# Attention weights: scores computed twice, places in rows, maxima subtracted by a product

## The chip, the cores and the metric

The kernel runs on one core of a Trainium2 chip. Its time is the device time of one execution in microseconds. Before the change the median of three runs is 446.92 us (446.77 to 449.26). The core's engines have their own instruction queues and run beside each other, held together by semaphores: PE (TensorE, matrix products and transposes into PSUM), DVE (VectorE), ACT (ScalarE), POOL (GpSimd) and SP (SyncE, which issues DMAs).

## The reference, cut to what matters

Sixteen batches of 128 rows and 128 features attend to a context of 77 places with 96 features, in 16 heads of 8. Then each row goes four times through two of four experts. All is float32.

```python
def _L0_xattn_ref(x, y, Wq, bq, Wkv, bkv, Wo, bo):      # x: (16, 128, 128), y: (16, 77, 96)
    q = (jnp.einsum('bld,ed->ble', x, Wq) + bq).reshape(b, l, h, dh)         # h = 16, dh = 8
    kv = (jnp.einsum('bmc,ec->bme', y, Wkv) + bkv).reshape(b, m, h, 2 * dh)
    k, v = (kv[..., :dh], kv[..., dh:])
    att = jax.nn.softmax(jnp.einsum('blhd,bmhd->blmh', q, k) * scale, axis=2)
    out = jnp.einsum('blmh,bmhd->blhd', att, v).reshape(b, l, d)
    return jnp.einsum('bld,ed->ble', out, Wo) + bo
...
x = x + jnp.tanh(g_xattn[0]) * _L0_xattn_ref(_layernorm(x, axis=-1), ctx_768, ...)
x = x + jnp.tanh(g_ffn[0]) * _L0_ffn_ref(_layernorm(x, axis=-1), ...)   # 4 rounds, top 2 of 4 experts
```

## The kernel before

There are two stages. The attention runs over the 16 batches `b`, one round of a loop for each (from L1072). Then the expert layers run over the rows in two halves and four rounds (`phase`, L1169), after the rows of a half were sorted by their experts: they are stored one tile at a time by indirect DMAs from POOL (`scatter`, L511) and loaded again by SP (`load`, L529). The first half is batches 0 to 7; its routing (`gate`, `count`, `route`, `places`) is spread over rounds 7 to 11, its eight stores over rounds 11 to 14, each held behind a DVE instruction of a list named `beats`.

The order on PE, DVE and ACT is the order of the program text (L80). POOL's own steps called through `gp` keep the program's order too. So each engine works through its instructions in line, and an instruction that waits holds up all behind it on its engine.

A round of the loop before:

- `spread_keys` (L765) on POOL, two batches ahead: the keys of a batch, 128 features by 77 places, times a mask, so that `km` holds four copies, each with one head of four left in (128 x 308).
- `turn_weights` (L816): the weights `ex`, query rows by heads and places, are transposed on PE head by head (16 transposes, 128x77 to 77x128, into `ps_tr`), and ACT copies each four of them to `exT`. It is called for groups 0 and 1, then after the next batch's scores for groups 2 and 3.
- `scores` (L778) of the next batch: four products, each on 32 of the 128 rows of PE, two to a PSUM tile of two banks (`sc`).
- Extra steps from lists by round (L953 to L976): for the next group of four batches `turn_ctx` (transposes of the context), `keys`, `turn_x` (transposes of the normalised rows), `queries` and `values`. `early` steps stand before the scores, `extra` ones behind them, `behind` ones at the round's end.
- `weights` (L797): for each half of the heads DVE takes the maximum over the places (`mx`) and subtracts it (`ex`), ACT takes the exponential.
- `put_out` (L848) of the batch before: the output projection into `ps_o`, and its sum with the residual on DVE.
- `attend` (L823): into `ps_av`, half 0 the sums of the weights (by `one`), half 1 the weighted values (by `vm`), each as four products in turn for each of four column groups, with the 77 places as PE's rows.
- `over_sums` (L841): a reciprocal and a product on DVE.

PSUM has eight banks: `p_m` two of one bank (L103), used by `ps_av` and the extra steps; `p_tr` two of one bank, used by `ps_tr` and `ps_o`; `p_sc` two tiles of two banks for the scores. A tile that takes a buffer waits until the reads of the tile before in it are done.

Ahead of the loop (L859 to L896) the first batches are prepared; `warm` and `warm_tr` are products of zeros in between.

## Time and profile before

| what | us |
|---|---|
| time, median of three runs | 446.92 |
| the profiled execution's own time | 444.04 |
| its span, first to last instruction | 442.3 |
| PE busy | 427.3 (97%) |
| DVE busy | 343.7 (78%) |
| ACT busy | 275.7 (62%) |
| POOL busy | 216.7 (49%) |
| 256 transposes of weights on PE, `ps_tr` | 35.1, 280 ns each with overlap |
| 64 copies of them on ACT, `exT` | 34.0, 582 ns each |
| 32 maxima on DVE, `mx` | 25.3, 790 ns each |
| 32 subtractions on DVE, `ex` | 25.4, 794 ns each |
| 32 exponentials on ACT, `ex` | 22.8, 718 ns each |

The granted clock is 0.993 of full speed over the span. Busy times are sums over the whole span, and a PE instruction is shown longer than the time until the next can start, so the sum of its durations is more than its busy time. First attend: 17.2 us after the start; the last begins at 107.4 us; the first product of the expert layers stands at 110.97 us. The stages have different limits, so the chain of waits (what released each step, followed back from the end) is read by stage.

### The profile page before, as it was taken

What the parts mean: (1) busy time and instruction counts of PE and PEld (TensorE: products, weight loads), DVE (VectorE), ACT (ScalarE), POOL (GpSimd) and SP (SyncE); (2) the same over time, 40 slices, a digit from 0 to 9 for tenths busy, and PEclk for the clock granted to TensorE, in tenths of its full rate; (3) what the DMA queues carried; (4) which work ended last, traced back from release to release, by engine and by line L of the source; (5) the groups of instructions that cost most, each with busy time, mean ns of one, the idle gap of its engine ahead of it and who ended that gap; (6) DMA issues with size and microseconds to landing.
All of it is one profiled execution on the core that took longest, in us unless ns stands there. A gap on an engine that the chain in (4) does not pass through costs nothing.

```text
span 442.3 us, 12215 instructions
## 1 busy us (share of the span) xinstructions
PE 427.3 (97%) x4492; PEld 403.8 (91%) x4492; DVE 343.7 (78%) x918; ACT 275.7 (62%) x857; POOL 216.7 (49%) x251
## 2 busy tenths in 40 slices
PE   9899999998999999999999999999999999999991
PEld 8678788876999999999999999999999999999991
DVE  7599989999667996887698589758867986764561
ACT  3677766756565666666566656656666665666661
POOL 6197824174025915852682475258326814650061
PEclk9999999999999999999999999999999999999997
DMA  6520000014002301400130131023011301400010
GB/s 164 189 99 3 3 1 1 4 63 136 2 27 75 99 1 63 137 2 26 66 108 1 50 99 50 1 76 124 1 37 63 100 2 63 146 31 9 1 33 16
DMA packets 19711, 24.08 MB, mean 54 GB/s; under 512 B 4099, under 2 KB 16708, under 8 KB 19524
## 3 DMA queue, kind: packets, MB, share of 16 engines
q1 hardware_dynamic: 15444, 13.43, 9.7%
q0 software_dynamic: 3584, 9.70, 6.2%
q8 instruction: 36, 0.59, 0.6%
q10 hardware_dynamic: 624, 0.17, 0.2%
q14 instruction: 23, 0.19, 0.1%
HBM read 13.58 MB, written 9.71 MB: 53 GB/s over the span
## 4 chain that ended last, share of the span: by engine, by line
PE 72%; issue 9%; DVE 9%; POOL 6%; DMA 2%; ACT 1%; POOLq 0%; DVEq 0%; SPq 0%; ACTq 0%
PE ps_y L255 28%; PE ps_h L255 28%; POOL out_dram L1156 4%; PE ps_av L255 3%; PE ps_tr L258 3%; DVE mx L803 2%; DVE ex L807 2%; PE ps_c L258 2%; DVE rs L843 1%; PE sc L255 1%; PE ps_warm L255 1%; PE ps_bh L255 1%; DMA rows<-sorted 1%; DMA sorted<-rows,pos_i 1%; POOL rows L93 1%
## 5 line engine op out<-in xcount | busy, mean ns | idle before, releaser
L1128 ACT ACTIVATE hT<-ps_h,wb 128x128 f32<-128x128 f32 x512 | 146.4, 369 | 81.2 <-ACT hT L1128 56.4
L255 PE MATMUL ps_h<-curT,wb 128*128 128x128 f32 x1024 | 135.4, 275 | 0.7 <-ACT curT L372 0.7
L255 PE MATMUL ps_y<-wb,hT 128*128 128x128 f32 x1024 | 135.7, 276 | 0.0
L255 PEld LDWEIGHTS ps_h<-curT,wb 128*128 128x128 f32 x1024 | 124.6, 192 | 0.9 <-ACT curT L372 0.9
L515 POOL DMA_INDIRECT sorted<-rows,pos_i x64 | 70.0, 1093 | 112.2 <-DVE start L508 49.3
L255 PEld LDWEIGHTS ps_y<-wb,hT 128*128 128x128 f32 x1024 | 124.5, 192 | 0.0
L1048 DVE COPY wb<-wall 128x1028 f32 x128 | 104.7, 820 | 13.1 <-issue 6.8
L93 POOL TENSOR_TENSOR lp<-rows,wg_rows 128x512 f32<-128x512 f32 x48 | 75.2, 1592 | 29.8 <-DVE rows L1142 27.3
L1142 DVE SCALAR_TENSOR_TENSOR rows<-ps_y,pws,rows 128x128 f32<-128x128 f32 x126 | 43.6, 346 | 34.0 <-PE ps_y L255 34.0
L1128 ACT ACTIVATE hT<-ps_h,wall 128x128 f32<-128x128 f32 x160 | 45.7, 368 | 32.5 <-PE ps_h L255 32.5
L255 PE MATMUL ps_y<-wall,hT 128*128 128x128 f32 x320 | 43.1, 278 | 0.0
L255 PE MATMUL ps_h<-cx,wall 128*128 128x128 f32 x320 | 42.3, 275 | 0.0
L821 ACT COPY exT<-ps_tr 77x512 f32<-77x512 f32 x64 | 34.0, 582 | 12.2 <-PE ps_tr L258 11.9
L255 PEld LDWEIGHTS ps_y<-wall,hT 128*128 128x128 f32 x320 | 38.9, 192 | 2.7 <-ACT hT L1128 2.7
L255 PEld LDWEIGHTS ps_h<-cx,wall 128*128 128x128 f32 x320 | 38.9, 192 | 0.0
L258 PEld LDWEIGHTS ps_tr<-ident,ex 128*77 128x77 f32 x256 | 27.9, 147 | 11.0 <-ACT exT L821 8.4
L258 PE MATMUL ps_tr<-ident,ex 128*77 128x128 f32 x256 | 35.1, 280 | 2.1 <-ACT exT L821 2.1
L1156 POOL DMA_INDIRECT out_dram<-res,id_i x16 | 18.6, 1160 | 35.8 <-DVE res L1147 31.8
L412 DVE TENSOR_REDUCE lg<-lp 128x4 f32<-128x512 f32 x48 | 32.3, 674 | 3.6 <-POOL lp L93 3.6
L813 ACT ACTIVATE ex<-ex 128x616 f32<-128x616 f32 x32 | 22.8, 718 | 13.7 <-DVE ex L807 13.5
L803 DVE TENSOR_REDUCE mx<-sc 128x8 f32<-128x616 f32 x32 | 25.3, 790 | 2.5 <-PE sc L255 2.5
L807 DVE TENSOR_TENSOR ex<-sc,mx 128x616 f32<-128x616 f32 x32 | 25.4, 794 | 1.4
(181 smaller groups left out, 450.5 us busy)
## 6 DMA issues: line engine op xcount, KB each, us to landing
rows<-sorted SPq DMA_DIRECT2D x16, 528.0 KB
wall<-in_L_ffn_W_dram SPq DMA_DIRECT2D x1, 1024.0 KB
wall<-in_L_ffn_W_dram SPq DMA_DIRECT2D x4, 256.0 KB
wg_rows<-wg_turned SPq DMA_DIRECT2D x1, 1024.0 KB
sorted<-rows,pos_i POOLq DMA_INDIRECT x64, 2.7
x_sb<-in_x_dram SPq DMA_DIRECT2D x3, 256.0 KB
ctx_sb<-in_ctx_dram SPq DMA_DIRECT2D x4, 115.5 KB
out_dram<-res,id_i POOLq DMA_INDIRECT x16, 2.3
```

Source lines behind the costliest of these rows:

```text
L93: return lambda *a, **kw: tc.keep_in_program_order(f(*a, **kw))
L255: nc.tensor.matmul(*args, **kw)
L258: nc.tensor.transpose(*args)
L412: nc.vector.tensor_reduce(lgs[h][:, t, :], prods.pop((h, t)), AX.X, ALU.add)
L515: ins = nc.gpsimd.indirect_dma_start(out=sorted_rows[h], out_offset=bass.IndirectOffsetOnAxis(ap=pos_i[:, t : t + 1], axis=0), in_=rows[h] ...
L803: beats.append(nc.vector.tensor_reduce(mx, sv, AX.X, ALU.max))
L807: nc.vector.tensor_tensor(eu.rearrange("l (g h) m -> l g h m", h=HG), sv, mx.unsqueeze(3).to_broadcast([P, 2, HG, M]), ALU.subtract,)
L821: nc.scalar.copy(exT[:, ts(g, HG), :].rearrange("m h l -> m (h l)"), ps[:M, :])
L1048: nc.vector.tensor_copy(wb, wall[:, ds(e, 1), :].rearrange("p o n -> p (o n)"))
L1128: nc.scalar.activation(hT[:, fc, :], ps[:, ts(fc, P)], AF.Gelu_apprx_tanh, bias=wb[:, W_B + fc : W_B + fc + 1],)
L1142: return nc.vector.scalar_tensor_tensor(at, y, w, at, ALU.mult, ALU.add)
L1156: ins = nc.gpsimd.indirect_dma_start(out=out_rows, out_offset=bass.IndirectOffsetOnAxis(ap=id_i[:, t : t + 1], axis=0), in_=res, in_offset ...
```

## The change

The weights are no longer subtracted and transposed. The scores are computed once as before, query rows by places, and only their maxima are taken (`maxima`), into a 128x128 tile `mxs` in which the heads of a group stand at columns 32 g. One transpose (`turn_maxima`, `ps_mx`) and a copy give `mxT`. Then `weights` computes the scores again with places in PSUM's rows, and a second product into the same sum, of a matrix `less` of minus ones and zeros with `mxT`, takes the maxima off. ACT takes the exponentials from PSUM straight into `exT`.

The 77 places are split into 64 and 13. The first 64 of two heads make 128 rows; the other 13 of eight heads make 104 rows (`values_left`, `vr`, `one_r`). So `attend` has three products in turn for each column group instead of four. The context's transpose `ctxT` is kept in two buffers for one group of four batches and holds the first 64 places twice and the last 13 eight times (two copies on ACT); `values` makes eight copies instead of four.

The pool `p_tr` is gone, `p_sc` has three tiles instead of two, and `ps_o` and `ps_mx` are taken from `p_m`. The maxima are taken two batches ahead of attend instead of one, `spread_keys` three ahead, and extra steps move by up to a round.

```diff
-    p_tr = scope.enter_context(tc.tile_pool(name="p_tr", bufs=2, space=PSUM))
-    p_sc = scope.enter_context(tc.tile_pool(name="p_sc", bufs=2, space=PSUM))
+    p_sc = scope.enter_context(tc.tile_pool(name="p_sc", bufs=3, space=PSUM))
...
+    def values_left(i, ps=None, eng=None):
+        if ps is None:
+            ps = bank("ps_vr")
+        for j in range(BB):
+            mm(ps[: HR * MR, ts(j, D)], ctxT[i % 2][:, j, 2 * MP : CT], wvT, ...)
+        v = ps[: HR * MR, :].rearrange("m (b d) -> m b d", d=D)
+        if eng is None:
+            eng = gp
+            left = awork.tile([HR * MR, BB, D], F32, tag="left", name="left", bufs=1)
+            nc.scalar.copy(left, v)
+            v = left
+        eng.tensor_tensor(vr[i % 2], v, one_r.unsqueeze(1).to_broadcast(...), ALU.mult)
...
     def scores(b, km):
...
-                mm(sc[:, g, : HG * M], q[at, :], km[at, :, :]..., start=True, stop=True)
+                dst = sc[:, g, : HG * M].rearrange("l (h m) -> l h m", m=M)
+                left = HG * MP + g * HG * MR
+                for m0, m1, lo in ((0, MP, 0), (MP, M, left)):
+                    mm(dst[:, :, m0:m1], q[at, :], km[at, lo : lo + HG * (m1 - m0)]..., ...)
...
+    def maxima(b, scs, then=None):
+        mx = mxs[b % 2].rearrange("l (t c) -> l t c", c=GW)
+        for u, sc in enumerate(scs):
+            if u and then:
+                then()
+            beats.append(nc.vector.tensor_reduce(mx[:, ts(u, 2), 0:HG], sc..., AX.X, ALU.max))
+
+    def turn_maxima(b):
+        ps = bank("ps_mx")
+        tp(ps[:, :L], mxs[b % 2], ident)
+        mxT = awork.tile([P, L], F32, tag="mxT", name="mxT")
+        nc.scalar.copy(mxT, ps[:, :L])
+        return mxT
+
+    def weights(b, km, mxT):
+        q = qT[b // BB][:, ts(b % BB, L)]
+        scs = [banks2("scT") for _ in range(2)]
+        def product(dst, at, cols):
+            mm(dst, km[at, cols], q[at, :], start=True, stop=False)
+            mm(dst, less[at, cols], mxT[at, :], start=False, stop=True)
+        for j in range(HP):
+            for half in range(2):
+                for g in range(NG):
+                    at = slice(g * GW, (g + 1) * GW)
+                    cols, dst = ts(j, P), scs[g // 2][:, g % 2, ts(j, L)]
+                    if half == 0:
+                        mm(dst, km[at, cols], q[at, :], start=True, stop=False)
+                    else:
+                        mm(dst, less[at, cols], mxT[at, :], start=False, stop=True)
+        n = HR * MR
+        for u in range(2):
+            product(scs[u][:n, 0, ts(HP, L)], slice(u * P // 2, (u + 1) * P // 2), slice(KW - n, KW))
+        exT = awork.tile([P, 2 * TB + 2 * L], F32, tag="exT", name="exT")
+        for u, sc in enumerate(scs):
+            nc.scalar.activation(exT[:, ts(u, TB)]..., sc[:, :, 0 : HP * L], AF.Exp, scale=scale)
+            nc.scalar.activation(exT[:n, 2 * TB + u * L : ...], sc[:n, 0, ts(HP, L)], AF.Exp, scale=scale)
+        return exT
...
     for b in range(B):
-        if b + 2 < B and b + 2 not in kms:
-            kms[b + 2] = spread_keys(b + 2)
-        exT = awork.tile([M, NH, L], F32, tag="exT", name="exT")
-        turn_weights(ex[b], exT, (0, 1))
+        if b + 3 < B:
+            kms[b + 3] = spread_keys(b + 3)
+        if b + 1 < B:
+            exTs[b + 1] = weights(b + 1, kms.pop(b + 1), mxT)
         for f in early[b]:
             f()
-        if b + 1 < B:
-            scs = scores(b + 1, kms.pop(b + 1))
-        turn_weights(ex.pop(b), exT, (2, 3))
+        if b + 2 < B:
+            scs = scores(b + 2, kms[b + 2])
         for f in extra[b]:
             f()
 
         def put_before(b=b):
             if b:
-                put_out(b - 1, o.pop(b - 1), bank_tr)
+                put_out(b - 1, o.pop(b - 1), bank)
 
-        if b + 1 < B:
-            ex[b + 1] = weights(scs, put_before)
+        if b + 2 < B:
+            maxima(b + 2, scs, put_before)
...
-        ps_av = attend(b, exT)
+        ps_av = attend(b, exTs.pop(b))
...
         o[b] = over_sums(ps_av)
+        if b + 2 < B:
+            mxT = turn_maxima(b + 2)
```

Ahead of the loop the changed kernel also makes `less` and the masks for 13 places, and takes the maxima of batches 0 and 1, the weights of batch 0, and the values of the first group, these by DVE instead of ACT. The steps `spread_rows` and `residual(0)` move behind the normalisation of the second group in round 0. The expert layers are the same text.

## The prediction

> **What bounds the kernel now.** I read the page's busy shares first, then cut the span where the work changes, because the change touches only the attention. That is what runs up to about 111 us; after it come the expert layers, which the change leaves alone. The table by stretch (busy us and instruction counts of PE, PEld, DVE, ACT and POOL, then the granted clock):

> ```profile
> 0.00:24.00 24.00, 20.77 (x200) 17.36 (x200) 16.75 (x44) 12.68 (x32) 10.09 (x23) 1.00 0.58 163
> 24.00:61.00 37.00, 36.99 (x632) 29.98 (x635) 34.50 (x77) 26.79 (x55) 26.91 (x82) 1.00 0.09 31
> 61.00:101.00 40.00, 39.32 (x630) 31.76 (x622) 37.29 (x95) 26.29 (x51) 18.27 (x21) 1.00 0.07 23
> 111.00:442.00 331.00, 322.19 (x2888) 318.38 (x2888) 246.16 (x687) 203.49 (x711) 156.63 (x121) 0.99 0.15 51
> ```

> At most 111 of 442.3 us can change. There PE and DVE are both near full, so which one ends a round has to be read from the chain of waits. From 24 to 61 us it is PE, without a gap; one round (batch 5):

> ```profile
> 43.71 1.03 PE ps_tr L258 x8
> 44.74 0.73 PE sc L255 x8
> 45.47 1.03 PE ps_tr L258 x8
> 46.50 0.52 PE ps_k L255 x2
> 47.02 0.22 PE ps_o L255 x2
> 47.24 1.91 PE ps_av L255 x64
> ```

> The reader is to see a round of 5.44 us that is PE work only: 4.92 for the batch and 0.52 for keys. From about 70 to 101 us the chain is DVE's instead:

> ```profile
> 83.85 0.72 DVE mx L803
> 84.61 0.04 issue
> 84.66 0.80 DVE ex L807
> 85.46 0.71 DVE mx L803
> 86.17 0.26 DVE rows L852
> 86.42 0.70 DVE ex L807
> ...
> 87.54 0.85 DVE rs L843
> ```

> A round there is 5.85 us (the chain's ps_av reciprocal stands at 81.69 and 87.54). At the end the first half's rows must be stored, sorted and loaded before the expert layers can begin:

> ```profile
> 102.06 3.54 DMA sorted<-rows,pos_i
> 105.74 3.86 DMA rows<-sorted
> 109.60 0.04 issue
> 109.64 0.67 PE ps_c L258 x4
> ```

> The last attend ends at 110, so these 7.4 us are covered almost exactly.

> **What goes.** Durations from here on are means of the costliest groups, shapes kept apart. Per batch: 16 transposes, 2.06 us of PE; four exT copies of 0.58, 2.3 us of ACT; two subtractions of 0.79, 1.6 us of DVE. DVE's round of 5.2 (two maxima, two subtractions, reciprocal 0.94, oT 0.29, rows 0.34, statistics 0.46) falls to 3.6 and bounds nothing any more. Attend falls from 16 rounds of four column groups to 12: 1.91 x 12/16 = 1.43.

> **What comes, one round on PE.** The maxima's transpose takes 0.27 to its end, its copy on ACT 0.27 (the 128x128 copy of wqT), hand-overs 0.1: the first product with the maxima starts 0.64 after the previous attend, with four score products in its shade. Three more groups of four products follow, two passes each. Four row groups side by side took 0.73 for two passes of 308 columns, 0.15 for one of 128: 6 x 0.15 = 0.9. The products for the left 13 places use half the rows: 8 passes, by ps_o's 0.11 a pass 0.44 (halves side by side) to 0.88 (in line); I take 0.55, and 0.1 for each change of shape (ps_av's 64 passes at 0.11 for each four make 1.75 of its 1.91). Sum 2.2. The scores for the maxima are now 64 + 13 places: 16 passes instead of 8. They also lose half of their neighbours: p_sc has three buffers for four tiles a round, so the second half of the scores takes the banks of the first weights tile and waits for its two exps. Each half is then two row groups alone: two passes of 256 columns and two of 52, by ps_k's 0.26 for 308 columns and a floor of 0.11: 0.65, with the switch 0.75. The exps start when the left product is through, last 0.6 + 0.3 (0.72 for 616 columns and 0.37 for 128, scaled) and end about when the first half does. So 2.2 + 0.75 + 0.1 + 0.75, ps_o 0.3, attend 1.45: 5.55 us, against 4.92. Even bare, PE's round is 0.6 longer.

> The scores could cost more. ps_k's rows put 308 columns at 0.26 a pass, and eight such passes of sc took 0.73, not 2.1, so row groups run abreast when each has one product. The changed code issues two of one group back to back (64 and 13 places), which no row here shows. The bounds: halves of two groups abreast, 1.5 in all as above, or every group alone, 4 x 0.65 = 2.6, a round 1.1 longer. I take the first: it is nearer to sc's row.
> [...]

> **Where PE then waits.** The changed program has no p_tr pool: ps_o, ps_av, ps_mx and every extra step share the two banks of p_m, and PE runs in program order. ACT begins four exps (1.8 us) when the weights are done, and the extras' copies queue behind them. By kind of round, in the changed order:
> - Keys: ps_k 0.52, the kT copy 0.42, then attend, which wants that bank: 5.55 + 0.52 + 0.6 = 6.7. Before: 5.44.
> - Queries: ps_xt 0.44 and ps_q 0.86; the xnT copy (0.59) stands behind the exps, attend waits for the qT copy (0.69): 5.55 + 1.3 + 1.0 = 7.9.
> - Left values (new): 0.88, its copy 0.58 before attend's bank is free: 7.2.
> - Values: 0.88 and ps_ct 0.27; ps_o takes ps_v's bank and waits for eight copies (four of 0.26 before; eight smaller ones by 0.2, 1.7 in all) less what ps_ct covers: 1.4. Attend then waits for the DVE step that empties ps_o (0.34 and hand-overs, 0.55): 9.0.

> A group of four: 30.8. Before, batches 4 to 7 took 23.3 (reciprocal of batch 3 at 38.34, of batch 7 at 61.61): +7.5. Batches 8 to 11 were DVE's, 25.9 in all (61.61 to 87.54). They become 30.8 plus 2 for the routing's products, which PE now has to wait out: +7.

> **Start.** Before, the first reciprocal stands at 19.23. The new prologue, in PE's order, with the time at which each step is through: scores 0 at 9.8 (8.7 before; a second ctxT copy of 0.5 is in front, a second km step, and the passes); two maxima of 0.79, 11.4; their transpose and copy 0.64, 12.1; weights 0 take a buffer of scores 1, which maxima 1 must first empty (13.4), then 1.9: 15.3; ps_mx and ps_v, 16.6; eight copies on DVE at 0.2, 18.4; values_left, whose products wait for those copies since both use one tile, 19.4; weights 1, 21.2; its exps (1.8) in front of the qT copy (0.37), 23.5; scores 2, 24.4; ctx with two copies (0.27 + 0.58 + 0.51) and keys 0.52 with switches, 26.9; attend, 28.4: +9. Rounds 1 to 3 were 19.1 (19.23 to 38.34). Now the group's 7.9, 7.2 and 9.0 make 24.1; round 1 also starts its exps only after DVE's four statistics (1.8), the tanh and three small ACT copies and then needs POOL's four rows (3.1): +3 with its queue. So +8.

> **End.** Round 12 (keys are done) and 13 are bare, 14 has no scores, 15 no weights either: 6.2 + 5.6 + 3.9 + 3.2 = 18.9, against 22.6 before: -3.7. Last attend at 110 + 7.5 + 7 + 9 + 8 - 3.7 = 138. The cover of the 7.4 us at the end is gone, though: those two short rounds no longer hide it. In the changed order on POOL the last store stands behind four row normalisations of 0.79 (3.1), which came after it before. So the load lands some 6 after the last attend, where it was 0.5 early: +6.

> Of what moves besides, km's one step of 0.70 on POOL becomes two, about 1.0, a batch earlier than needed; POOL was busy 26.91 of 37 us in the first stretch and has room; if it had not, scores would wait for it 0.3 a round. The step spread_rows with its two DMAs moves behind norm_x; what it loads (wg_rows) is first read after 111 us: nothing.

> Added up: 9 + 8 + 7.5 + 7 - 3.7 + 6 = +34. Not everything will fall late at once; I take +33. The profiled execution's 444.04 us (span 442.3) would become 477; it lies 2.9 under the median of the runs, so the median goes from 446.92 to **480**.

> **Rivals.**
> 1. *PE never waits* (the other side, not slower). ACT and DVE have 2.3 and 1.6 us less a round; if their copies land before PE wants the banks, a round is its work: 0.2 + 1.9 + 0.9 + 0.25 + 1.43 = 4.7, extras of 3.9 for each four batches. From a first attend at 22 (without the prologue's waits), 13 rounds of 4.7 + 1.0, two short ones of 3, 2 for routing: 104, and with the end's 6 the layers begin at 110. That is 446 us, no change, and a few us under if the end is covered too. For it: DVE's chain from 70 us. Against: the waits are in the program, and the bank of ps_v alone costs 1 us a group. It decides if the exps and the copy behind them end before attend is reached. 10%.
> 2. *Row groups in line*: 15 rounds 1.1 longer, +16: 496. For it: the back-to-back products. Against: sc's 0.73 for eight passes. 18%.
> 3. *Half the waits*: the copies on ACT come in between the exps' gaps and the left products run abreast. 16 x 0.6 for the bare rounds plus half of the other 24: about +20, 467. 12%.

> **Numbers.** My case 60%. The range runs from 462 (under the third rival) to 500 (over the second); outside it I leave the first rival and a little at the top. One per cent, 4.5 us, is about what can be told from no change here: three runs before spread over 2.5. Rival 1 splits into 0.06 faster and 0.04 same; all else is slower, 0.90.

> **What would show it.** In the new profile: first reciprocal near 28, rounds of 6.5 to 9 us with PE idle before ps_o and ps_av until ACT copies (vm, left, kT, qT) end; DVE under 60% of the stretch; scores in two halves with exT's exp before the second; the last store behind POOL's rows. PE without idle and rounds under 5.5 us would prove me wrong; scores of over 1.3 us a half would show rival 2.

## The result, and the profile after

| | median us | runs | ratio to before, 95% interval |
|---|---|---|---|
| before | 446.85 | 446.71 to 449.26 | |
| after | 491.38 (of four runs; a fifth took 487.41) | 487.41 to 497.16 | 1.0951 (1.0886 to 1.1016) |

The change makes the kernel 9.5% slower by the ratio; the medians differ by 44.5 us. The ratio leaves out the longest of the five runs, 497.16, as a slow one. The forecast was 480 with a range of 462 to 500, so the side and the range hold and the size is 11 us short. The profiled execution (span 495.4) is that longest run and has the lowest clock, 0.943; the other four have 0.960 to 0.974, and before has 0.993.

From the page of the profile after: busy time by engine, and the granted clock in 40 slices of 12.4 us.

```profile
span 495.4 us, 12827 instructions
...
PE 461.5 (93%) x4796; PEld 429.9 (87%) x4796; DVE 326.1 (66%) x901; ACT 253.6 (51%) x856; POOL 222.8 (45%) x275
...
PEclk9759989759998899999999999999999999999997
```

DVE fell from 78% to 66% and ACT from 62% to 51%, as the change intends; PE's busy time grew by 34 us, to which the last row adds a reason of its own: the granted clock dips to 7 and 5 tenths twice in the attention, where before it stood at 1.00. By stretch (busy us of PE, PEld, DVE, ACT and POOL, then the clock):

```profile
24.00:61.00 37.00, 30.43 (x394) 22.84 (x394) 14.75 (x39) 13.48 (x40) 17.44 (x57) 0.78 0.08 31
61.00:101.00 40.00, 35.94 (x545) 29.11 (x533) 19.12 (x49) 12.36 (x36) 17.92 (x39) 0.84 0.01 2
101.00:162.00 61.00, 51.38 (x800) 40.77 (x796) 33.84 (x89) 18.17 (x52) 22.34 (x29) 0.89 0.11 37
162.00:495.00 333.00, 323.99 (x2888) 320.02 (x2888) 246.58 (x687) 203.19 (x712) 153.10 (x121) 0.99 0.15 50
```

Between 24 us and the first expert layer PE was idle for 2.7 of 87 us before (36.99, 39.32 and, from 101 to 111 us, 7.99 busy); now it is for 20 of 138. No other engine is near full. So PE waits, and the chain of waits says for whom. Rounds 6 and 7 of after:

```profile
77.18 1.52 PE ps_av L294 x48
78.70 0.26 PE ps_mx L297
78.96 2.01 PE scT L294 x40
80.98 0.59 ACT exT L902
81.57 0.17 ACT exT L906
...
81.79 0.86 PE sc L294 x8
82.66 1.06 PE ps_vr L294 x8
...
83.80 0.59 ACT left L814
...
84.44 1.52 PE ps_av L294 x48
...
89.97 1.10 PE ps_v L294 x8
...
92.61 0.21 ACT vm L793
...
92.88 0.50 PE ps_o L294 x2
...
93.40 0.36 DVE rows L943
```

The reader is to see the round that was predicted: the second half of the scores (`sc` x8) stands behind the exponentials of the first weights tile, attend waits for the copy `left`, and in round 7 `ps_o` waits for the last of eight copies `vm`, which run from 91.09 to 92.83. What PE waited for from 24 to 162 us, in all (us, times, longest):

```profile
PE ps_o L294 <- ACT vm L793: 3.2, 2, 1.6
...
PE ps_av L294 <- DVE rows L943: 1.8, 4, 0.5
PE sc L294 <- ACT qT L783: 1.8, 2, 1.1
...
PE ps_av L294 <- ACT left L814: 1.5, 3, 0.5
```

The waits are those of the prediction. What it did not foresee follows them. Six stretches of after, in pairs: some 3.4 us with a wait, and what comes next (busy us of PE first; the clock is the third number from the end):

```profile
15.40:18.90 3.50, 1.71 (x18) 1.38 (x15) 1.66 (x8) 1.84 (x6) 0.00 (x0) 0.99 0.57 167
18.90:39.30 20.40, 17.87 (x168) 13.38 (x168) 5.63 (x17) 4.22 (x13) 2.23 (x3) 0.50 0.04 12
...
56.40:59.80 3.40, 1.79 (x16) 1.56 (x14) 0.00 (x0) 2.04 (x9) 2.55 (x13) 1.00 0.01 2
59.80:66.60 6.80, 6.36 (x91) 5.01 (x89) 3.24 (x9) 0.96 (x3) 1.86 (x5) 0.50 0.01 2
...
90.50:94.00 3.50, 1.50 (x19) 1.15 (x22) 0.60 (x2) 2.73 (x10) 0.00 (x0) 0.99 0.00 0
94.00:111.00 17.00, 16.57 (x190) 13.62 (x186) 6.84 (x19) 2.36 (x7) 7.86 (x12) 0.50 0.00 1
```

Each time PE is busy for about half of some 3.4 us, it runs at half clock for the next 7 to 20 us. The waits are 1.96 (left values of the start behind eight DVE copies), 1.61 and 1.55 us (`ps_o` behind the eight `vm` copies of rounds 3 and 7). This is not a trait of the longest run alone: in the trace of the run "scores alternate" below, which took 491.17, PE is busy for 1.44 of the 3.40 us from 17.4, behind the same eight DVE copies, and half clock follows for 3.4 us; between 57 and 66 and between 92 and 97 us, near the second and third of these pairs, it has 6.8 and 3.4 us at half clock.

My theory for the tests was therefore: (A) PE's order, by which it waits for shared banks and ACT's copies, costs about what was predicted, and (B) the granted clock that falls in these waits costs some 10 us more. Against them: the second scores and the maxima cost this much by PE's work alone, or (the prediction's second rival) row groups are worked in line.

### The profile page after: what moved, and what is told of

Read it like the earlier page. It is cut to its first block, busy times and chain, and to the rows that moved or that the text cites. A ratio compares the mean times of both kernels' runs of the same rounds, so it can differ in the third digit from the quotient of the medians.

```text
span 495.4 us, 12827 instructions
## 1 busy us (share of the span) xinstructions
PE 461.5 (93%) x4796; PEld 429.9 (87%) x4796; DVE 326.1 (66%) x901; ACT 253.6 (51%) x856; POOL 222.8 (45%) x275
## 4 chain that ended last, share of the span: by engine, by line
PE 76%; issue 9%; POOL 5%; ACT 5%; DVE 3%; ACTq 1%; DVEq 0%; POOLq 0%
PE ps_y L294 25%; PE ps_h L294 25%; PE scT L294 7%; PE ps_av L294 6%; POOL out_dram L1260 4%; PE sc L294 3%; PE ps_c L297 2%; ACT exT L902 1%; PE ps_v L294 1%; PE ps_mx L297 1%; PE ps_lg L294 1%; PE ps_k L294 1%; PE ps_o L294 1%; PE ps_bh L294 1%; ACT vm L793 1%
## 5 line engine op out<-in xcount | busy, mean ns | idle before, releaser
L554 POOL DMA_INDIRECT sorted<-rows,pos_i x64 | 65.8, 1027 | 117.8 <-DVE start L547 57.8
L93 POOL TENSOR_TENSOR lp<-rows,wg_rows 128x512 f32<-128x512 f32 x48 | 75.7, 1600 | 28.7 <-DVE rows L1246 27.1
L864 DVE TENSOR_REDUCE mx<-sc 128x8 f32<-128x616 f32 x32 | 25.2, 795 | 31.9 <-PE sc L294 31.9
L902 ACT ACTIVATE exT<-scT 128x512 f32<-128x512 f32 x32 | 19.2, 599 | 38.9 <-PE scT L294 38.9
L294 PEld LDWEIGHTS sc<-km,qT 32*128 32x128 f32 x256 | 20.3, 201 | 8.7 <-issue 3.2
L294 PE MATMUL scT<-qT,km 32*128 32x128 f32 (+1 forms) x320 | 26.4, 346 | 0.6 <-DVE mx L864 0.6
L294 PE MATMUL sc<-km,qT 32*128 32x52 f32 (+1 forms) x256 | 24.6, 356 | 2.5 <-ACT qT L783 1.8
L934 DVE RECIPROCAL rs<-ps_av 128x128 f32<-128x128 f32 x16 | 15.3, 955 | 17.1 <-PE ps_av L294 13.9
```

The lines of the kernel that those rows point to most:

```text
L93: return lambda *a, **kw: tc.keep_in_program_order(f(*a, **kw))
L294: nc.tensor.matmul(*args, **kw)
L554: ins = nc.gpsimd.indirect_dma_start(out=sorted_rows[h], out_offset=bass.IndirectOffsetOnAxis(ap=pos_i[:, t : t + 1], axis=0), in_=rows[h] ...
L864: beats.append(nc.vector.tensor_reduce(mx[:, ts(u, 2), 0:HG], sc[:, :, : HG * M].rearrange("l g (h m) -> l g h m", m=M), AX.X, ALU.max,))
L902: nc.scalar.activation(exT[:, ts(u, TB)].rearrange("p (g l) -> p g l", g=2), sc[:, :, 0 : HP * L], AF.Exp, scale=scale,)
L934: nc.vector.reciprocal(rs, ps[:, 0:L])
```

## The experiments

The runs came in four sets, each on one chip with the kernel before beside it: the first four of the table below, the next four, the next three, and the last. The kernel before took 444.1 in the first, second and fourth set, and 446.7 in the third, as beside the changed kernel; so across sets the ratios are compared. "Changed" below is the changed kernel. The clocks are means over the span, by the clock's own records; these begin only some us after the start (at 5.7 in the trace of before, at 5.2 in that of after), and the time ahead of the first one counts as full.

| run | median us | ratio to before (95%) | clocks |
|---|---|---|---|
| scores alternate | 491.15 | 1.1044 (1.1001 to 1.1087) | 0.954 to 0.967 |
| before, `ps_o` shared | 451.41 | 1.0171 (1.0152 to 1.0190) | 0.989 to 0.993 |
| no `less` products | 487.27 | 1.0938 (1.0871 to 1.1006) | 0.926 to 0.942 |
| no maxima | 463.54 | 1.0478 (1.0411 to 1.0544) | 0.930 to 0.950 |
| PE filled | 487.24 | 1.0993 (1.0926 to 1.1061) | 0.975 to 0.988 |
| store first | 484.73 | 1.0927 (1.0867 to 1.0987) | 0.957 to 0.974 |
| extras first | 480.65 | 1.0813 (1.0792 to 1.0833) | 0.964 to 0.967 |
| extras first, DVE copies | 476.63 | 1.0754 (1.0707 to 1.0802) | 0.964 to 0.980 |
| left values, own bank | 489.58 | 1.0956 (1.0909 to 1.1004) | 0.966 to 0.970 |
| own banks for `ps_o`, `ps_mx` | 495.06 | 1.1083 (1.0999 to 1.1167) | 0.943 to 0.961 |
| together | 472.26 | 1.0566 (1.0548 to 1.0585) | 0.985 to 0.988 |
| before, no zeros | 445.19 | 1.0024 (1.0012 to 1.0037) | 0.993 to 0.995 |

And by stretch, each from one trace (us; the marks are the starts of attend's reciprocals `rs` and of the first `ps_h`):

| | to first `rs` | rounds 1-3 | 4-7 | 8-11 | 12-15 | to `ps_h` | rest |
|---|---|---|---|---|---|---|---|
| before | 19.2 | 19.1 | 23.3 | 25.8 | 22.8 | 0.7 | 331.3 |
| after | 33.8 | 29.4 | 33.3 | 38.0 | 26.7 | 0.9 | 333.2 |
| scores alternate | 31.5 | 31.6 | 32.9 | 32.5 | 22.3 | 5.1 | 333.6 |
| before, `ps_o` shared | 19.4 | 20.6 | 25.4 | 28.8 | 23.0 | 0.9 | 331.3 |
| no `less` products | 32.3 | 29.3 | 31.6 | 36.8 | 20.0 | 4.9 | 333.7 |
| no maxima | 25.2 | 25.2 | 25.9 | 23.2 | 16.5 | 10.3 | 333.4 |
| PE filled | 30.6 | 30.6 | 31.1 | 34.1 | 23.2 | 5.3 | 331.3 |
| store first | 28.6 | 31.6 | 32.9 | 32.5 | 22.3 | 1.3 | 333.8 |
| extras first | 30.2 | 27.6 | 28.8 | 33.0 | 22.3 | 4.7 | 334.0 |
| extras first, DVE copies | 30.5 | 24.6 | 27.0 | 30.3 | 22.2 | 5.0 | 333.8 |
| left values, own bank | 28.3 | 30.2 | 32.6 | 34.8 | 26.1 | 3.2 | 333.1 |
| together | 28.4 | 26.5 | 27.1 | 30.3 | 27.4 | 0.9 | 331.6 |
| before, no zeros | 20.5 | 19.1 | 23.3 | 25.9 | 22.8 | 0.4 | 331.3 |

### Scores alternate between row groups

```diff
-            for g in range(2):
-                ...
-                for m0, m1, lo in ((0, MP, 0), (MP, M, left)):
+            for m0, m1 in ((0, MP), (MP, M)):
+                for g in range(2):
+                    ...
                     mm(dst[:, :, m0:m1], q[at, :], km[at, lo : ...]..., start=True, stop=True)
```

> The changed kernel with the score products in another order: the 64 places of both row groups first, then the 13 places of both, where the changed kernel issues both products of one row group back to back. If row groups are worked in line when two products of one group stand back to back (the rival of the prediction), alternating them lets them run abreast and wins up to 1 us in each of 16 rounds: 475 to 480 us instead of 491. If they run abreast already, as the trace of the changed kernel shows (a half of the scores 0.6 us), nothing changes: 488 to 494.

491.15, against 491.38 of the changed kernel. The rival falls: row groups run abreast whichever way the products are written. Where the two halves follow each other, the 16 passes take 1.19 us in after (from 73.86), so 0.6 for a half, and from 69 to 92 us the 48 score products last 204, 322 and 478 ns (shortest, median, longest) here as in after; a half that stands alone takes 0.86 to its end in both. This run also serves as a second sample of the changed kernel; its trace differs from the first in the clock (35 us at half instead of 57, the tail included) and in rounds 12 to 15.

### Before, with ps_o in the shared banks

```diff
-                put_out(b - 1, o.pop(b - 1), bank_tr)
+                put_out(b - 1, o.pop(b - 1), bank)
```

> The kernel before with one edit: the product ps_o takes its bank from the two of p_m, which it now shares with ps_av and all extra steps, and no longer from p_tr. No work is added. If PE's waits for banks that ACT or DVE have yet to empty are the main cost of the change, this alone costs a part of it: by hand, following the order of the program with the durations of the trace, 8 us, 455 us instead of 447, with PE idle before ps_o and ps_av. If banks are not what matters (the cost is the added work of PE), it stays within 2 us of 447.

7.3 us, 1.7% (1.5 to 1.9), where 8 were worked out. No work was added; PE's waits from 24 to 118 us now begin with this line, which the kernel before does not have:

```profile
PE ps_av L255 <- DVE rows L852: 5.0, 6, 1.7
```

So the sharing of two banks is a cost by itself, and the clock has no part in it here: it stays at 0.993.

### Without the products that take the maxima off

```diff
-            mm(dst, km[at, cols], q[at, :], start=True, stop=False)
-            mm(dst, less[at, cols], mxT[at, :], start=False, stop=True)
+            mm(dst, km[at, cols], q[at, :], start=True, stop=True)
```

> The changed kernel without the products that take the maxima off the scores (20 of 40 products of a weights step, the ones with the tile less); the scores for the maxima, the maxima and their transpose are still computed and then not used, so the softmax is taken without the maximum. It tells the price of these products and of the wait for the turned maxima. By hand, with the order of the program and full clock: 13 us less than the changed kernel, 478. If the bound is PE's own work, 16 times 1.0 us and the wait for mxT, 0.3 each: 20 less, 471. If ACT's chain (exps, then the copies) is what ends last in every round, the earlier exps move everything alike and it is also 13 to 20; if it changes by less than 5, the rounds are bound by something that does not begin with these products.

487.27, 4 less and not 13 to 20; the interval reaches that of the changed kernel. Half of the weights' products are gone, and the clock fell to 0.926 to 0.942. Its profile (same columns as above):

```profile
20.00:43.90 23.90, 21.28 (x196) 15.11 (x194) 7.86 (x22) 6.24 (x18) 8.22 (x17) 0.50 0.12 47
57.50:71.20 13.70, 13.18 (x144) 9.86 (x144) 6.00 (x16) 3.16 (x8) 8.16 (x17) 0.50 0.00 1
91.70:105.30 13.60, 13.17 (x131) 10.19 (x126) 5.31 (x15) 2.37 (x7) 6.86 (x10) 0.50 0.01 1
```

51 us at half clock in these three, where after has 44 (20.5 from 18.9, 6.8 from 59.8 and 17.1 from 94.0); by the program the same three waits stand ahead of them. By my expectation a change under 5 us meant that the rounds are bound by something else. The trace and the clocks show what it is: the half clock stayed at these places and grew, and work taken off PE was paid back in clock. How much of it, no run separates; an estimate: by their mean clocks these runs spend some 25 us more at half clock than those of "scores alternate", which at 0.28 us each (the fit further below) is 7, and 4 and 7 make 11 of the 13 worked out.

### Without the maxima

```diff
-    maxima(0, scs)
-    mxT = turn_maxima(0)
...
-        if b + 2 < B:
-            scs = scores(b + 2, kms[b + 2])
...
-            mm(dst, less[at, cols], mxT[at, :], start=False, stop=True)
```

> The changed kernel with the first scores, the maxima, their transpose and the products that take them off all left out: the softmax is taken without the maximum; all banks, copies and orders of the rest stay. By hand, at full clock: the first layer begins 33 us earlier than in the changed kernel, 458 us. If the waits behind ACT's copies for the two shared banks were the whole cost they would stay, and it would be near 475; if the doubled scores and the maxima's way through PE are the cost, it comes back to 447 to 455, still above before by the lost cover at the end (6).

463.54, between the two cases. The first scores, the maxima and what takes them off are worth 27.6 us, the larger part of the loss (the waits and the half clock that went with them included; the run does not separate these from PE's bare work), but without them the kernel is still 4.8% slower than before: by the table 12 us in the start and rounds 1 to 3, 9.6 at the end, 2 in the layers. There the last store stands behind POOL's four rows, as the prediction put it:

```profile
112.54 2.81 POOL rows L93
...
115.35 2.35 POOL rows L93 x3
...
117.86 2.55 DMA sorted<-rows,pos_i
...
120.56 3.73 DMA rows<-sorted
...
124.43 1.10 PE ps_c L297 x4
```

### Products of zeros where PE waits

```diff
+    def fill(ps, n):
+        for _ in range(n):
+            mm(ps[:, P : 2 * P], zero, zero, start=True, stop=True)
...
+        if b % 4 == 3 and b + 2 < B:
+            fill(scs[1][:, 1, 256:512], 5)
...
                 put_out(b - 1, o.pop(b - 1), bank)
+                if b + 2 < B:
+                    fill(scs[1][:, 1, 256:512], 2)
...
+            fill(banks2("ps_warm")[:, 0, :], 18)
             turn_half(0, 0, state[0]["c"])
```

> The changed kernel with products of zeros by zeros put into the places where PE waits in it: seven (128 columns, nobody reads them) between the values and the left values of the start, four between the contexts' transposes and the keys of round 0, five before ps_o in each round with values, two before ps_av in every round with scores, 18 before the load of the sorted rows. 72 in all, some 20 us of PE at 0.28 each, meant to lie in idle time. If the granted clock falls because PE waits (7 to 28 us at half clock after the waits of the start, the value rounds and the end), the clock comes back to 0.98 to 0.99, as before has it, and the time falls by 4 to 10 us, to 481 to 487, though work was added. If the clock falls for another reason, it stays at 0.95 to 0.97 and the time is 491 or some us more.

The clock came back to 0.987 and 0.988 in three of four runs, and the time fell by 4 us though 72 products were added. The same two places as in the pairs above, rounds 3 and 7:

```profile
55.80:59.20 3.40, 2.95 (x28) 2.76 (x26) 0.16 (x1) 2.34 (x10) 2.59 (x14) 1.00 0.01 2
59.20:66.00 6.80, 6.55 (x114) 5.27 (x113) 3.97 (x10) 2.26 (x7) 3.01 (x6) 1.00 0.02 5
...
86.50:90.00 3.50, 3.10 (x31) 2.85 (x28) 0.70 (x1) 2.48 (x10) 0.00 (x0) 1.00 0.00 0
90.00:110.00 20.00, 18.52 (x305) 14.95 (x303) 11.42 (x29) 6.12 (x16) 7.92 (x12) 1.00 0.01 2
```

With 2.95 and 3.10 us of PE in the step instead of 1.79 and 1.50, no half clock follows. The one that is left in the attention (37.2 to 44.0) follows waits that were not filled, 0.9 and 0.4 us in round 1 (PE busy for 2.35 of 3.50 us). So here it is the waits that pull the clock down (0.975 to 0.988 with them filled, 0.954 to 0.967 in "scores alternate"). The layers need 331.3 us again, as before: the 2.3 they lost were the half clock after the wait at the end (a clock of 0.61 from 156 to 162 us in "scores alternate", 1.00 here). The fall in time is smaller than its spread: the intervals of this run and of the one with alternating scores, 1.0993 and 1.1044, overlap.

### The last store ahead of POOL's rows

```diff
+    class Late:
+        def tensor_scalar(self, *a, **kw):
+            ins = gp.tensor_scalar(*a, **kw)
+            after(ins, stores[-1], "behind the last store")
...
-            early[B - 1] += [lambda i=i: norm_x1(i - 1, gp)]
+            behind[B - 1] += [lambda i=i: norm_x1(i - 1, Late())]
```

> The changed kernel with the four row normalisations on POOL put behind the last store of the sorted rows, instead of in front of it. The term 'end' of the prediction: the store starts 3.2 us earlier, the load lands 3 us earlier, and so does the first layer: 488 instead of 491 by the median, the gap between the last reciprocal and the first layer 2 us instead of 5.1. If the last store does not set the end (the load's own wait, PE's end), nothing changes: 490 to 492.

484.73; the interval lies below that of the run with alternating scores. The stretch to the first layer is 1.3 instead of 5.1. That is 3.8, a little over the 3 expected. The medians differ by 6.4; in the traces a start that was through 2.9 sooner makes up the rest, and the edit does not touch it. The starts of after and of this run show the clock's price on the same instructions. After:

```profile
19.07 2.03 PE ps_v L294 x8
21.11 3.19 PE scT L294 x40
```

This run:

```profile
19.07 1.12 PE ps_v L294 x8
20.19 1.77 PE scT L294 x40
```

Both begin at 19.07 us behind the same wait; one finds half clock, the other not (0.50 and 1.00 from 19 to 24 us). The first reciprocal then stands at 33.8 and at 28.6 us.

### The extra steps ahead of the scores

```diff
+        for f in soon[b]:
+            f()
         if b + 2 < B:
             scs = scores(b + 2, kms[b + 2])
...
-        extra[b + 2] += [lambda i=i: values_left(i)]
-        extra[b + 3] += [lambda i=i: values(i)]
+        soon[b + 2] += [lambda i=i: values_left(i)]
+        soon[b + 3] += [lambda i=i: values(i)]
```

(and the same for `turn_ctx` and `keys`; in the second run besides `eng=nc.vector` for the left values and `copy=nc.vector.tensor_copy` for the values)

> The changed kernel with four extra steps (contexts' transposes, keys, left values, values) ahead of the scores in their round instead of behind them. No work changes; their copies on ACT then stand in front of the second pair of exps instead of behind all of them, or have the scores as cover. If PE's waits for the shared banks are the cost, this wins a part of it: by hand, from the program's order with the trace's durations, 6 us, 485. If these waits are hidden anyway (the bound is PE's work), it stays at 491; if the exps now come late behind the copies, it is up to 5 us slower.

> As the run with the extra steps ahead of the scores, and besides the values' eight copies and the left values' product done by DVE, which has idle time, instead of ACT and POOL. By hand 3 us less again, 482, if ACT's queue in front of ps_o and ps_av is what PE waits for. If DVE's own order then holds up the maxima or the rows, it is no better than the run with the order alone, or worse.

480.65 and 476.63: 10.5 and 4 us for an order and a choice of engine, with no work taken away, more than the 6 and 3 worked out. Rounds 1 to 3 and 4 to 7 give 7.0 and 5.9 of it (31.6 to 24.6 and 32.9 to 27.0). This bears out (A): the same work, in another order and with DVE for some of ACT's copies, gives back a third of what the change lost. It also speaks against PE's work alone as the cost. The clock of the first run (0.964 to 0.967) is no higher than that with alternating scores, so its 10.5 us are order; that of the second reaches 0.980, so a part of its 4 can be clock.

### Left values in their own bank; own banks for ps_o and ps_mx

```diff
-    values_left(0, ps_v[:, 1, :], nc.vector)
+    values_left(0, None, nc.vector)
```

> The changed kernel with the left values of the start in a bank of their own (from p_m), no longer in the tile of the values; their products then need not wait for the eight copies out of that tile (1.96 us in the trace of the changed kernel, the longest wait of its start, and the one after which its profiled run shows 20 us at half clock). If such a wait is what pulls the clock down, the runs no longer show a half clock before the 30th us, the first reciprocal stands at 27 to 28 in the profiled run, and the median is 2 to 6 us under the changed kernel's 491. If only the wait's own length counts, 1 to 2 us. If PE waits as long at the next step (for the qT copy behind the exps), nothing.

In the trace the first reciprocal stands at 28.3 us. But the median is 489.58 and its interval that of the changed kernel (1.0909 to 1.1004 against 1.0886 to 1.1016): a miss. The clock is no higher (0.966 to 0.970, where the changed kernel has 0.960 to 0.974 without its longest run), so there was no less half clock.

```diff
+    p_tr = scope.enter_context(tc.tile_pool(name="p_tr", bufs=2, space=PSUM))
-    p_sc = scope.enter_context(tc.tile_pool(name="p_sc", bufs=3, space=PSUM))
+    p_sc = scope.enter_context(tc.tile_pool(name="p_sc", bufs=2, space=PSUM))
```

> The changed kernel with two banks of a pool of their own for ps_o and the turned maxima, as ps_o and the transposes had before, and the scores' pool back at two tiles of two banks, so that each weights step waits for the maxima of the scores and each scores step for the exps. If sharing p_m is the cost of the change, it is up to 8 us faster (483). By hand, from the program's order with the trace's durations: the waits move from p_m to p_sc, and it is 4 us slower, 495. Near 491 would say that the two cancel.

495.06, as worked out; its interval touches that of the changed kernel, so only the 483 is excluded. The largest sum among PE's waits from 24 to 158 us now stands in front of the scores. The profile names no releaser; by the program it is the exponential that has to empty the tile first.

```profile
PE sc L298 <- issue: 4.7, 5, 0.9
```

### Together

The edits of the runs "extras first, DVE copies", "store first" and "left values", and 14 products of zeros in round 0 and at the end.

> The changed kernel with the edits that won put together: the extra steps ahead of the scores with the values' copies on DVE (476.6 alone), the last store ahead of POOL's rows (6 less alone), the left values of the start in their own bank, and 14 products of zeros where PE waits in round 0 and at the end. If the gains add up: 476.6 - 6 - 2 - 2 = 466 to 468, with a clock over 0.98. If they share one cause (the clock, at the end above all), 470 to 473. If PE's order is the bound, whatever the waits, it stays above 474. In no case under 447: what stays is a start of some 27 instead of 19 us, rounds of 6.5 to 7 against 5.8, and 4 us less cover.

472.26, ratio 1.0566: the best of the changed kernels, and 5.7% slower than before. It is in the middle case, 5 us over the sum of the gains. The 5 us are rounds 12 to 15: 27.4 against 22.2 in the trace of "extras first, DVE copies". In those rounds of this trace PE waits for `mxT` 3.4 us in two places (2.4 the longest), and in the trace of "left values, own bank", which has the same, ACT's copy begins 1.8 us after the modelled end of the transpose that it copies. The traces of after and of the three runs of the third set have such rounds, those of the first and second sets do not. What delays the hand-over was not settled.

### Before, without its products of zeros

```diff
-    warm(6)
...
-    warm_tr(1)
...
-    warm_tr(4)
```

> The kernel before without its 19 products of zeros by zeros (two records each, 275 ns, between 1 and 11.5 us of its start, which nobody reads); all else stays. It is the counterpart of the run that fills PE's waits in the changed kernel. If PE's idle time is what pulls the granted clock down, the start of the kernel before, too, now shows a half clock after the 10th us, over 3 to 20 us, and the time grows by 2 to 8 us (449 to 455 where before is 447), with a clock of 0.97 to 0.985 over the span instead of 0.993. If the clock follows something that only the changed kernel has (its small products in row groups, its banks), the clock stays at 0.993 and the time within 1 us, or falls by the products' own 1 to 2 us.

The time grows by 1.1 us, though 19 products are gone. The mean clock reads 0.993 to 0.995, but what lies ahead of the clock's first record (at 5.7 us in the trace of before) counts as full. There the products themselves show the clock. Before:

```profile
9.67 1.04 PE L255 MATMUL ps_v<-wvT,ctxT 97*77 97x128 f32 x8
11.44 1.04 PE L258 MATMUL ps_tr<-ident,ex 128*77 128x128 f32 x8
```

Without its products of zeros:

```profile
10.80 1.91 PE L255 MATMUL ps_v<-wvT,ctxT 97*77 97x128 f32 x8
12.51 1.92 PE L258 MATMUL ps_tr<-ident,ex 128*77 128x128 f32 x8
...
15.16 1.10 PE L258 MATMUL ps_tr<-ident,ex 128*77 128x128 f32 x8
```

In the trace of after a 128x128 product takes 421 ns where the records show 0.50 (from 162.2 to 165.6 us) and 272 to 275 behind it; in the trace of before it takes 421 up to 5.7 us and 272 to 275 from there on. Eight products in 1.9 us instead of 1.0 are nearly the ratio of eight of `ps_h` in 2.08 and 1.16 us, at 0.50 in after and at full clock in before. So both runs start at half clock, and without the products of zeros it lasts some 9 us longer, to about 15 by the rows above; PE is busy for 4.75 of the first 9 us instead of 7.96. The first reciprocal stands at 20.5 instead of 19.2. This is on the side of (B), but smaller than was expected (2 to 8 us), and no new half clock comes behind it: the clock reads 1.00 from 16 to 24 us, where PE is busy for 2.94 and 3.48 of each 4 us.

## Why the prediction was right, and where not

The mechanism was right. The named waits are in the trace, PE's new order is the bound, DVE and ACT have room and it does not help, and the three rivals are gone: PE waits (first), the row groups run abreast (second: a half of the scores takes 0.6 us, and the start times at the end of this document show products of different row groups side by side), and the waits are whole, not half (third). By its terms, with the run "scores alternate" as the ordinary sample of the changed kernel:

| term | forecast | scores alternate | after's trace | PE filled |
|---|---|---|---|---|
| start | +9 | +12.3 | +14.6 | +11.4 |
| rounds 1-3 | +8 | +12.5 | +10.3 | +11.5 |
| rounds 4-7 | +7.5 | +9.6 | +10.1 | +7.9 |
| rounds 8-11 | +7 | +6.6 | +12.2 | +8.3 |
| rounds 12-15 | -3.7 | -0.5 | +3.9 | +0.4 |
| end | +6 | +4.4 | +0.2 | +4.5 |
| layers | 0 | +2.3 | +1.9 | 0.0 |
| sum | +34 | +47.2 | +53.2 | +44.0 |

Two things are mis-sized. (Two rows of the prediction's list are also added up too high: 5.55 + 0.88 + 0.58 is 7.0 and not 7.2, and 5.55 + 0.88 + 0.27 + 1.4 + 0.55 is 8.65 and not 9.0. That makes each group of four 0.5 us too long, against the direction of the miss.)

*The clock is missing from the sum.* The durations are those of the profile before, nearly all at full clock, and the text has no word on what waits do to the clock. In nine runs of the changed kernel and of the one with alternating scores, which does the same work in the same time, the span grows by 0.28 us with each microsecond at half clock (correlation 0.9; half-clock time is twice the lost share of the clock times the span; without the longest run 0.22 and 0.7). Carried to the 7 us that the records of before have, all of them in its tail, the line gives 481. So of a usual 489 some 8 us are clock, and of after's 495.4 some 14. The line is a fit over few runs, and the price by "PE filled" is lower (4 us, with the products of zeros in it), so 4 to 8.

*Two terms of the order are too small.* At full clock 481 less 442.3 is +39 instead of +34. Rounds 12 to 15 win nothing: round 15 takes 5.7 instead of the forecast 3.2, since `ps_o` of round 14 then waits 1.4 for DVE's reciprocal and product, with no other work of PE left to cover it. And rounds 1 to 3 cost 2 to 4.5 more: for the second group the queries stand ahead of the scores in round 2, with the left values, and not in round 1, so the wait for `qT` (1.1) adds to a full round. The start was right at full clock: 28.4 forecast, and 28.6 in the trace of "store first", whose clock reads 1.00 up to 24 us ("left values" has 28.3, and "together", with other edits in its start, 28.4). In "scores alternate", with 31.5, six products of zeros from 9.42 us take 1.27, where eight take 0.89 from 12.61 on, so the half clock of the start lasts until the first scores; these begin at 10.7 instead of 8.7, and 3.4 us at half clock follow from 20.8.

What was said of the groups in the middle held: rounds 4 to 7 were forecast at 6.7, 7.9, 7.2 and 9.0, and take 6.8, 7.5, 7.3 and 9.6 where PE was filled. The bank of `ps_o`, argued but not priced alone, costs 7.3 in the kernel before. The end was right in its cause (POOL's rows ahead of the last store), and in its size within 2 us.

## What to carry to other kernels

Before a change that moves work from a full engine into an in-order queue, list for each step the bank it needs and whose copy empties that bank: here the order of four extra steps was worth 10.5 us, and two shared banks 7.3, with no work changed. A wait of PE is not paid by its own length alone: where PE was busy for only half of some 3.4 us, what followed ran at half clock for 3.4 to 20.5 us in the trace of after, so a sum made at full clock is a lower bound as soon as the change adds such waits. And work taken off PE while its waits stay can come back as clock, as the run without the `less` products suggests.

## What was not expected of the hardware

In the trace of after the second half's products of 256 columns begin (74.188 and 74.201) before the products of 52 columns of the first half (74.400), which stand ahead of them in the program, in other row groups. The order between row groups is not that of the program there.
